# Layer 0 attention: every weight transposed on VectorE, and half of the minimum's input folded on GpSimd

## The chip, the cores and the metric

The kernel runs on one core of a Trainium2 chip. Five engines run side by side, each in the order of its own instruction list: TensorE (PE, with its weight loads shown as PEld), VectorE (DVE), ScalarE (ACT), GpSimd (POOL) and SyncE (SP), which here only issues DMAs. They meet at semaphores. The metric is the device time of one execution in microseconds (us).

## The reference

The whole program is a stack of four layers on an input of 2 x 256 channels x 1024 pixels. Only the attention of layer 0 is touched:

```python
qf = q.reshape(B * Hq * Wq_sp * NUM_HEADS, dk) / scale
kf = k.reshape(-1, dk)
vf = v.reshape(-1, dv)
A = jax.nn.softmax(qf @ kf.T, axis=1)
O = A @ vf
```

Queries and keys of both images and all four heads are thrown together: 8192 queries of 64 numbers against 8192 keys. After that come two more attentions, an additive attention and two mixtures of experts (layers 1 to 3), which are the same in both kernels.

## The kernel before

`layer0` normalises the input, projects it to `qT`, `kT` and `v`, and calls `shared_attention`, which is a software pipeline written out by hand. Queries are taken 32 positions at a time (`S` = 32), which makes 64 rows (`rows`), and each row is worked in four units (`units` = 256): `m` counts units, `i = m // 4` is the row, `p` picks a pair of heads, `h` picks half of the keys. One unit holds two score tiles of 128 x 1024, for r = 0 and r = 1 (the two heads of the pair). The softmax needs one minimum for a query (queries carry a minus sign), spread over four groups of 32 partitions.

What happens to a unit, in the order of its life:

- `score(m)`: 16 matmuls (L145; the trace has two instructions for each, 32) put the two tiles into PSUM. The pool `p_a` of tile r = 0 has two buffers, the pool `p_b` of tile r = 1 has one. DVE copies tile 0 to SBUF and takes its minimum on the way (L152); ACT copies tile 1 (L155). The copies (`sc0`, `sc1`) have 7 buffers each.
- `reduce(m)`: DVE takes the minimum of tile 1 over its 1024 columns (L166). After the second unit of a pair (h = 1), `gather` sends four small DMAs on SP's queue (L161), which bring the minima of the four partition groups side by side into `sa_got`.
- `spread_least(k)`: DVE reduces `sa_got` to `sa_min` (L172), and four DMAs on SP (L175) copy the result to all partition groups as `sa_shift`.
- `weigh(m)`: ACT takes the exponential of both tiles in place with `sa_shift` as bias (L182), and sums it.
- `turn(m)`: DVE transposes the first 768 of the 1024 columns of both tiles in blocks of 32 x 32 (L195). `turn_late(m)`: PE transposes the last 256 columns (L203, four instructions) into PSUM, and ACT copies them out to `wl` (L204).
- `value(m)`: 16 matmuls (32 instructions, L221) multiply weights and values into `sums`. Columns that PE transposed come out in another order, so they need values in that order too, `v_odd`, which `layer0` makes ahead of the attention (L364 to L377: four GpSimd copies, 32 PE instructions, 8 DVE additions).
- Once in a row: the sums of the weights are gathered with four DMAs (from `weigh`, `sa_sums`), inverted (`invert`, L228, L229, and L232 on GpSimd), spread by a matmul (L238) and copied by ACT (L243). `done` multiplies them in on DVE (L394); every eighth row it also projects the output (L400, L405).

A manual schedule fixes the order on every engine. At step n the calls are issued in the order of the loop at the end of `shared_attention`, each for a unit some steps back. Before, that loop calls `done(n-13)`, `reduce(n-1)`, `turn(n-6)`, `weigh(n-5)`, `score(n)`, `turn_late(n-6)`, `spread_least` of the pair that ended at n-2, `invert(n-10)`, `value(n-9)` and `spread(n-12)`. So a pair of units 2k and 2k+1 has its last `reduce`, with the gather, in step 2k+2, and its `spread_least` in step 2k+3. In that step the DVE has `reduce(2k+2)`, two transposes and the copy of the scores before it comes to the reduction that needs the gathered minima.

Of the kernel before, what the change touches and what calls it, by code (L numbers as in the profile page):

```python
# [19 lines left out]
F32 = mybir.dt.float32  # L20
# [3 lines left out]
ALU = mybir.AluOpType  # L24
AX = mybir.AxisListType
PSUM = bass.MemoryType.PSUM

P = 128
B, C, N = 2, 256, 1024
T = B * N  # L30
NT = T // P
CC = C // P
CH = 512
# [36 lines left out]
class Stack:  # L70
# [34 lines left out]

    def shared_attention(self, qT, kT, v, v_odd, ctx, done):

# [7 lines left out]


        tc, nc = self.tc, self.nc
        S, G, B, LATE = 32, P // 32, N // 32, 8
        DIRECT = (B - LATE) * S
        rows = T // S
        units = 4 * rows
        psum = lambda name, bufs: ctx.enter_context(tc.tile_pool(name=name, bufs=bufs, space=PSUM))
        p_a, p_b, p_o, p_t = psum("sa_a", 2), psum("sa_b", 1), psum("sa_o", 1), psum("sa_t", 1)
        sb = ctx.enter_context(tc.tile_pool(name="sa_sb", bufs=2))
        keys = kT.rearrange("p n (b c i) -> p n b c i", c=G, i=S)  # L130
        ones = sb.tile([S, P], F32, name="ones", bufs=1)
        nc.gpsimd.memset(ones, 1.0)
        names = "least got shift total parts scores weights late sums rec norm"
        least, got, shift, total, parts, scores, weights, late, sums, rec, norm = ({} for _ in names.split())

        def score(m):
            i, p, h = m // 4, m // 2 % 2, m % 2
# [19 lines left out]
        def gather(t, n, name):  # L157
# [3 lines left out]
                nc.sync.dma_start(out=g[:, :, c, :], in_=t[S * c : S * (c + 1)])  # L161
            return g.rearrange("q n c h -> q n (c h)")

        def reduce(m):
            h = m % 2
            nc.vector.tensor_reduce(least[m // 2][:, 1, h : h + 1], scores[m][1], AX.X, ALU.min)  # L166
            if h == 1:
                got[m // 2] = gather(least.pop(m // 2), 2, "sa_got")

        def spread_least(k):  # L170
            t = self.small.tile([S, 2], F32, name="sa_min")
            nc.vector.tensor_reduce(t, got.pop(k), AX.X, ALU.min)  # L172
            shift[k] = self.small.tile([P, 2], F32, name="sa_shift")
            for c in range(G):
                nc.sync.dma_start(out=shift[k][S * c : S * (c + 1)], in_=t)  # L175

        def weigh(m):
            i, p, h = m // 4, m // 2 % 2, m % 2
            if m % 4 == 0:
                total[i] = self.small.tile([P, 4, 2], F32, name="sa_total")  # L180
            for r in range(2):
                nc.scalar.activation(  # L182
                    scores[m][r], scores[m][r], AF.Exp, bias=shift[m // 2][:, r : r + 1], scale=-1.0,
                    accum_out=total[i][:, 2 * p + r, h : h + 1],
                )
            if m % 4 == 3:
                parts[i] = gather(total.pop(i), 4, "sa_sums")

        def turn(m):
            i, p, h = m // 4, m // 2 % 2, m % 2  # L190
            if p == 0:
                weights[i, h] = sb.tile([P, 4, DIRECT], F32, name="wt", bufs=3)
                late[i, h] = sb.tile([P, LATE // 4, 4, P], F32, name="wl", bufs=3)
            for r in range(2):
                nc.vector.transpose(weights[i, h][:, 2 * p + r, :], scores[m][r][:, :DIRECT])  # L195

        def turn_late(m):
            i, p, h = m // 4, m // 2 % 2, m % 2
            ps = p_t.tile([P, LATE // 4, 2, P], F32, name="ps_t")
            for r, s in enumerate(scores.pop(m)):  # L200
                for g in range(LATE // 4):
                    at = DIRECT + g * P
                    nc.tensor.transpose(ps[:, g, r, :], s[:, at : at + P], self.ident)  # L203
            return lambda: nc.scalar.copy(late[i, h][:, :, 2 * p : 2 * p + 2, :], ps)  # L204

        def value(m):
            i, h, j = m // 4, m // 2 % 2, m % 2
            if h == 0 and j == 0:
                sums[i] = p_o.tile([P, 4, S], F32, name="ps_o")
            for t in range(B // 4):  # L210
                for k in range(2):
                    b = B // 2 * k + B // 4 * j + t
                    at = B * h + b
                    if b < B - LATE:
                        values = v[:, at % NT, 64 * (at // NT) : 64 * (at // NT + 1)]
                        w = weights[i, h][:, :, S * b : S * (b + 1)]
                    else:
                        g, c = t // G, t % G
                        values = v_odd[:, h, t, :]
                        w = late[i, h][:, g, :, S * c : S * (c + 1)]  # L220
                    nc.tensor.matmul(  # L221
                        sums[i][64 * k : 64 * (k + 1)], lhsT=values, rhs=w,
                        start=(h == 0 and j == 0 and t == 0), stop=(h == 1 and j == 1 and t == B // 4 - 1),
                    )

        def invert(i):
            t, r = (self.small.tile([S, 4], F32, name=f"sa_{n}") for n in ("tot", "rec"))
            nc.vector.tensor_reduce(t, parts.pop(i), AX.X, ALU.add)  # L228
            nc.vector.reciprocal(r, t)  # L229
            rec[i] = sb.tile([S, 4, S], F32, name="diag")  # L230
            shape = [S, 4, S]
            nc.gpsimd.tensor_tensor(  # L232
                rec[i], self.ident[0:S, 0:S].unsqueeze(1).to_broadcast(shape), broadcast(r, shape), ALU.mult
            )

        def spread(i):
            ps = p_t.tile([P, 4, S], F32, name="ps_n", tag="ps_t")
            nc.tensor.matmul(  # L238
                ps.rearrange("p n q -> p (n q)"), lhsT=ones, rhs=rec.pop(i).rearrange("p n q -> p (n q)"),
                start=True, stop=True,  # L240
            )
            norm[i] = sb.tile([P, 4, S], F32, name="norm")
            nc.scalar.copy(norm[i], ps)  # L243

        with tc.manual_schedule():
            for n in range(units + 14):
                on = lambda d: 0 <= n - d < units
                row = lambda d: on(d) and (n - d) % 4 == 0
                if row(13):
                    i = (n - 13) // 4  # L250
                    done(i, sums.pop(i), norm.pop(i), p_t)
                if on(1):
                    reduce(n - 1)
                if on(6):
                    turn(n - 6)
                if on(5):
                    weigh(n - 5)
                if on(0):
                    score(n)
                if on(6):  # L260
                    turn_late(n - 6)()
                if on(3) and (n - 3) % 2 == 0:
                    spread_least((n - 3) // 2)
                if row(10):
                    invert((n - 10) // 4)
                if on(9):
                    value(n - 9)
                if row(12):
                    spread((n - 12) // 4)

    def layer0(self, xT):
        tc, nc = self.tc, self.nc
        with ExitStack() as ctx:
            w = ctx.enter_context(tc.tile_pool(name="l0_w", bufs=1))
            big = ctx.enter_context(tc.tile_pool(name="l0_big", bufs=1))


            qT = big.tile([P, CC, T], F32, name="qT")  # L280
            kT = big.tile([P, 4, T], F32, name="kT")
            v = big.tile([P, NT, C], F32, name="v")
            v_odd = big.tile([P, 2, 8, 64], F32, name="v_odd")

            with tc.tile_pool(name="l0_xn", bufs=1) as xp, tc.tile_pool(
                name="l0_ps", bufs=4, space=PSUM
# [74 lines left out]
                    nc.vector.tensor_tensor(v[:, i, :], ps, bv, ALU.add)  # L361


                late = xp.tile([P, CC, 2, 4, 4, 32], F32, name="late")  # L364
                runs = xn[:, :, N:].rearrange("p c (g b r i) -> p c g b r i", g=2, b=4, r=4)
                for c in range(CC):
                    for g in range(2):
                        nc.gpsimd.tensor_copy(late[:, c, g].rearrange("p r b i -> p b r i"), runs[:, c, g])
                for t in range(8):
                    ps = psum.tile([P, C], F32, name="ps_v", tag="ps_row")  # L370
                    for c in range(CC):
                        nc.tensor.matmul(
                            ps, lhsT=late[:, c, t // 4, t % 4].rearrange("p b i -> p (b i)"), rhs=wv[:, c, :],
                            start=(c == 0), stop=(c == CC - 1),
                        )
                    odd = lambda a: a.rearrange("p (h r d) -> p h r d", h=2, r=2)[:, :, 1, :]
                    nc.vector.tensor_tensor(v_odd[:, :, t, :], odd(ps), odd(bv), ALU.add)  # L377


            zero = big.tile([P, C], F32, name="zero")  # L380
            nc.gpsimd.memset(zero, 0.0)
            for slots in self.slots_in:
# [21 lines left out]
                    x = xT[:, o, t * C : (t + 1) * C]  # L404
                    nc.vector.scalar_tensor_tensor(x, ps, bo[:, o : o + 1], x, ALU.add, ALU.add)  # L405

            self.shared_attention(qT, kT, v, v_odd, ctx, done)

    def pool_stats(self, pool, psum, mv, average, tag="ps_row"):

# [1445 lines left out]
```

## Time and profile before

| what | us |
|---|---|
| median of 3 timed runs | 2989.76 (2987.06 to 2990.24) |
| the profiled execution, its time | 2959.93 |
| the profiled execution, its span | 2958.2 |
| from the first score matmul to the last output of layer 0's attention | 67.6 to 1275.4 |
| busy in the whole span: PE, DVE, ACT, POOL | 2756.9, 1952.9, 1945.6, 429.5 |

The profile is of one execution, and all durations below come from it. A row of the trace shows the start, the duration, the engine, the line in the kernel, the operation, output and input tiles with their shapes, and in brackets how long the engine sat idle before it and what ended that. An instruction starts before the one ahead of it has fully ended, so the spacing from start to start is what one instruction costs a busy engine, and is less than its duration. PE's busy time counts modelled ends and doesn't say that it works at its peak.

Layer 0's attention takes some 41% of the span.

### The profile page before, as it was taken

The numbers are of one execution on the slowest core, as the hardware profiler recorded it, in microseconds if no ns is written. First come the engines' busy times: TensorE is split into PE (matmuls) and PEld (weight loads), VectorE is DVE, ScalarE is ACT, GpSimd is POOL, SyncE is SP. The second block draws the span as 40 slices with busy tenths as digits, with TensorE's granted clock in tenths as the row PEclk, the third lists the DMA queues.
The fourth block names the chain that finished last, engine by engine and source line by source line (L and its number), as shares of the span: only waits on it lengthen the run. The fifth ranks groups of instructions, "written<-read, shape, count | busy, mean of one in ns | idle before, by whom it ended". The sixth has DMA issues, their size and how long they took to land. (4 is left out here: it accounts for less than half of the span.)

```text
span 2958.2 us, 78693 instructions
## 1 busy us (share of the span) xinstructions
PE 2756.9 (93%) x33062; PEld 1743.4 (59%) x33062; DVE 1952.9 (66%) x3650; ACT 1945.6 (66%) x2941; POOL 429.5 (15%) x538
## 2 busy tenths in 40 slices
PE   7999999999999999979999968699999999999997
PEld 4465656666666656655565445499866634355586
DVE  5898989898989898847778956663522234224242
ACT  1787878787878887825555522121199898998732
POOL 4000000000000000000111123433411120302142
PEclk9999999999999999989999988799999999999998
DMA  3000000000000000011101010243312210312254
GB/s 130 2 3 3 3 3 3 3 3 3 3 3 3 3 3 3 3 48 31 27 14 31 6 27 1 95 161 107 116 64 64 69 35 1 146 58 85 94 196 126
DMA packets 180578, 131.46 MB, mean 44 GB/s; under 512 B 130992, under 2 KB 162368, under 8 KB 173056
## 3 DMA queue, kind: packets, MB, share of 16 engines
q0 software_dynamic: 29232, 81.71, 8.3%
q1 hardware_dynamic: 149552, 44.27, 6.7%
q8 instruction: 259, 4.24, 0.6%
q14 instruction: 95, 0.78, 0.1%
q10 hardware_dynamic: 1440, 0.47, 0.1%
HBM read 181.24 MB, written 29.49 MB: 71 GB/s over the span
## 5 line engine op out<-in xcount | busy, mean ns | idle before, releaser
L182 ACT ACTIVATE sc<-sc,sa_shift 128x1024 f32<-128x1024 f32 x512 | 585.2, 1148 | 54.3 <-DMA sa_shift<-sa_min 54.1
L1641 ACT ACTIVATE th<-kT,qb 128x1024 f32<-128x1024 f32 x512 | 539.6, 1134 | 49.7 <-PE ps_e L1650 43.6
L145 PE MATMUL ps_s<-kT,qT 64*32 64x512 f32 x8192 | 505.0, 597 | 9.2 <-ACT sc L155 8.5
L221 PE MATMUL ps_o<-wt,v 128*64 128x128 f32 x6144 | 503.2, 276 | 0.0
L221 PEld LDWEIGHTS ps_o<-wt,v 128*64 128x64 f32 x6144 | 442.1, 137 | 42.7 <-issue 42.7
L195 DVE STREAM_TRANSPOSE wt<-sc 128x768 f32<-128x768 f32 x512 | 465.7, 943 | 0.9 <-ACT sc L182 0.9
L155 ACT COPY sc<-ps_s 128x1024 f32<-128x1024 f32 x256 | 257.4, 1005 | 117.9 <-PE ps_s L145 43.7
L1423 PEld LDWEIGHTS ps_h<-xe,ew 128*128 128x128 f32 x2320 | 276.1, 194 | 56.6 <-issue 32.8
L166 DVE TENSOR_REDUCE sa_least<-sc 128x1 f32<-128x1024 f32 x256 | 306.1, 1196 | 1.6 <-ACT sc L155 1.5
L152 DVE TENSOR_SCALAR_CACHE_REDUCE sc<-ps_s 128x1024 f32<-128x1024 f32 x256 | 301.3, 1177 | 6.4 <-PE ps_s L145 6.4
L1650 PE MATMUL ps_e<-th,pick 128*32 128x512 f32 x2048 | 299.5, 611 | 5.8 <-DVE sc_a L1657 4.4
L1423 PE MATMUL ps_h<-xe,ew 128*128 128x128 f32 x2320 | 292.1, 280 | 7.9 <-DVE xe L1406 7.9
L1443 PE MATMUL ps_y<-ew,h 128*128 128x256 f32 x1160 | 271.5, 383 | 3.5 <-DVE y L1447 2.1
L221 PE MATMUL ps_o<-wl,v_odd 128*64 128x128 f32 x2048 | 251.8, 276 | 0.0
L1443 PEld LDWEIGHTS ps_y<-ew,h 128*128 128x128 f32 x1160 | 212.9, 190 | 60.7 <-issue 18.8
L145 PEld LDWEIGHTS ps_s<-kT,qT 64*32 64x32 f32 x8192 | 126.8, 106 | 201.0 <-issue 169.0
L203 PEld LDWEIGHTS ps_t<-ident,sc 128*128 128x128 f32 x1024 | 107.8, 141 | 216.5 <-issue 168.6
L649 ACT ACTIVATE sc<-sc,l_least 128x1024 f32<-128x1024 f32 x128 | 146.7, 1147 | 126.9 <-DVE sc L636 126.5
L221 PEld LDWEIGHTS ps_o<-wl,v_odd 128*64 128x64 f32 x2048 | 221.2, 137 | 0.0
L1434 DVE TENSOR_TENSOR hb<-ps_h,ew 128x512 f32<-128x512 f32 x115 | 79.4, 690 | 198.2 <-PE ps_h L1423 172.3
L232 POOL TENSOR_TENSOR diag<-ident,sa_rec 32x128 f32<-32x128 f32 x64 | 24.9, 390 | 1172.1 <-DVE sa_rec L229 1172.1
L1412 ACT ACTIVATE h<-hb 128x512 f32<-128x512 f32 x115 | 71.5, 623 | 183.8 <-DVE hb L1434 183.6
(292 smaller groups left out, 3483.7 us busy)
## 6 DMA issues: line engine op xcount, KB each, us to landing
xr<-slots_in SPq DMA_DIRECT2D x99, 128.0 KB, 2.8
slots_out<-y SPq DMA_DIRECT2D x99, 128.0 KB, 1.7
sa_got<-sa_least SPq DMA_DIRECT2D x512, 0.5 KB, 1.8
sa_shift<-sa_min SPq DMA_DIRECT2D x512, 0.2 KB, 1.7
slots_in<-zero POOLq DMA_DIRECT2D x46, 128.0 KB, 2.2
sa_sums<-sa_total SPq DMA_DIRECT2D x256, 1.0 KB, 1.8
kh<-kh SPq DMA_DIRECT2D x32, 128.0 KB, 2.3
qh<-qh SPq DMA_DIRECT2D x32, 128.0 KB, 2.3
```

The source lines that it names most:

```text
L145: nc.tensor.matmul(ps[r][S * c : S * (c + 1), a, :].rearrange("p (b i) -> p b i", i=S), lhsT=qT[half, p, S * i : S * (i + 1)], rhs=keys[ha ...
L152: nc.vector.tensor_scalar(scores[m][0], flat[0], 1.0, None, ALU.mult, ALU.min, accum_out=least[m // 2][:, 0, h : h + 1])
L155: nc.scalar.copy(scores[m][1], flat[1])
L166: nc.vector.tensor_reduce(least[m // 2][:, 1, h : h + 1], scores[m][1], AX.X, ALU.min)
L182: nc.scalar.activation(scores[m][r], scores[m][r], AF.Exp, bias=shift[m // 2][:, r : r + 1], scale=-1.0, accum_out=total[i][:, 2 * p + r, ...
L195: nc.vector.transpose(weights[i, h][:, 2 * p + r, :], scores[m][r][:, :DIRECT])
L221: nc.tensor.matmul(sums[i][64 * k : 64 * (k + 1)], lhsT=values, rhs=w, start=(h == 0 and j == 0 and t == 0), stop=(h == 1 and j == 1 and t ...
L649: nc.scalar.activation(scores[n][r], scores[n][r], AF.Exp, bias=least[n][:, r : r + 1], scale=-1.0, accum_out=total[n // 4][:, at : at + 1],)
L1423: nc.tensor.matmul(ps[:, j, :], lhsT=a[:, c, at : at + P], rhs=x[:, c, :], start=(c == 0), stop=(c == CC - 1),)
L1443: nc.tensor.matmul(ps, lhsT=h[:, j, :], rhs=w2[:, j, :], start=(j == 0), stop=(j == HB - 1))
L1641: nc.scalar.activation(h, keys, AF.Tanh, bias=self.qb[b][:, s // G, g : g + 1])
L1650: nc.tensor.matmul(pe[i][c * U : (c + 1) * U, a, :], lhsT=self.pick[:, k, :], rhs=h[:, a, :], start=(k == 0), stop=(k == G - 1),)
```

## The change

All 1024 columns are transposed on DVE; `turn_late`, the PSUM tile it used, ACT's copy of it, `wl` and `v_odd` go. In their place GpSimd folds tile 1 of each unit in half: for the left half a and the right half b it computes a - min(max(a - b, 0), 3e38), which is the smaller of the two, in three instructions of 128 x 512. DVE's `reduce` then runs over 512 columns and not over 1024. In the schedule `fold(n)` stands right after `score(n)`; `reduce` moves from n-1 to n-3 and behind the score; `spread_least` moves to the pair that ended at n-3, and all later calls move back by one step.

```diff
+        def fold(m):
+            x = scores[m][1]
+            a, b = x[:, :CH], x[:, CH:]
+            folded[m] = y = sb.tile([P, CH], F32, name="fold", bufs=3)
+            nc.gpsimd.tensor_tensor(y, a, b, ALU.subtract)
+            nc.gpsimd.tensor_scalar(y, y, 3.0e38, 0.0, ALU.min, ALU.max)
+            nc.gpsimd.tensor_tensor(y, a, y, ALU.subtract)
+
         def reduce(m):
             h = m % 2
-            nc.vector.tensor_reduce(least[m // 2][:, 1, h : h + 1], scores[m][1], AX.X, ALU.min)
+            nc.vector.tensor_reduce(least[m // 2][:, 1, h : h + 1], folded.pop(m), AX.X, ALU.min)
             if h == 1:
                 got[m // 2] = gather(least.pop(m // 2), 2, "sa_got")
...
             if p == 0:
-                weights[i, h] = sb.tile([P, 4, DIRECT], F32, name="wt", bufs=3)
-                late[i, h] = sb.tile([P, LATE // 4, 4, P], F32, name="wl", bufs=3)
-            for r in range(2):
-                nc.vector.transpose(weights[i, h][:, 2 * p + r, :], scores[m][r][:, :DIRECT])
-
-        def turn_late(m):
...
+                weights[i, h] = sb.tile([P, 4, N], F32, name="wt", bufs=3)
+            for r, x in enumerate(scores.pop(m)):
+                nc.vector.transpose(weights[i, h][:, 2 * p + r, :], x)
...
-            for n in range(units + 14):
+            for n in range(units + 15):
...
-                if row(13):
-                    i = (n - 13) // 4
+                if row(14):
+                    i = (n - 14) // 4
                     done(i, sums.pop(i), norm.pop(i), p_t)
-                if on(1):
-                    reduce(n - 1)
+                if on(7):
+                    turn(n - 7)
                 if on(6):
-                    turn(n - 6)
-                if on(5):
-                    weigh(n - 5)
+                    weigh(n - 6)
                 if on(0):
                     score(n)
-                if on(6):
-                    turn_late(n - 6)()
-                if on(3) and (n - 3) % 2 == 0:
-                    spread_least((n - 3) // 2)
-                if row(10):
-                    invert((n - 10) // 4)
-                if on(9):
-                    value(n - 9)
-                if row(12):
-                    spread((n - 12) // 4)
+                    fold(n)
+                if on(3):
+                    reduce(n - 3)
+                if on(4) and (n - 4) % 2 == 0:
+                    spread_least((n - 4) // 2)
+                if row(11):
+                    invert((n - 11) // 4)
+                if on(10):
+                    value(n - 10)
+                if row(13):
+                    spread((n - 13) // 4)
```

More of the change, by code (lines that the diff above doesn't have):

```diff
@@ L104, in rsqrt, with shared_attention @@
         return r
-    def shared_attention(self, qT, kT, v, v_odd, ctx, done):
+    def shared_attention(self, qT, kT, v, ctx, done):
         tc, nc = self.tc, self.nc
-        S, G, B, LATE = 32, P // 32, N // 32, 8
-        DIRECT = (B - LATE) * S
+        S, G, B = 32, P // 32, N // 32
         rows = T // S
@@ L132, in shared_attention @@
         nc.gpsimd.memset(ones, 1.0)
-        names = "least got shift total parts scores weights late sums rec norm"
-        least, got, shift, total, parts, scores, weights, late, sums, rec, norm = ({} for _ in names.split())
+        names = "least folded got shift total parts scores weights sums rec norm"
+        least, folded, got, shift, total, parts, scores, weights, sums, rec, norm = ({} for _ in names.split())
         def score(m):
@@ L191, in turn @@
             if p == 0:
-                weights[i, h] = sb.tile([P, 4, DIRECT], F32, name="wt", bufs=3)
-                late[i, h] = sb.tile([P, LATE // 4, 4, P], F32, name="wl", bufs=3)
-            for r in range(2):
-                nc.vector.transpose(weights[i, h][:, 2 * p + r, :], scores[m][r][:, :DIRECT])
-        def turn_late(m):
[L198 to L204, printed above, removed]
+                weights[i, h] = sb.tile([P, 4, N], F32, name="wt", bufs=3)
+            for r, x in enumerate(scores.pop(m)):
+                nc.vector.transpose(weights[i, h][:, 2 * p + r, :], x)
         def value(m):
@@ L213, in value @@
                     at = B * h + b
[L214 to L220, printed above, removed]
                     nc.tensor.matmul(
-                        sums[i][64 * k : 64 * (k + 1)], lhsT=values, rhs=w,
+                        sums[i][64 * k : 64 * (k + 1)],
+                        lhsT=v[:, at % NT, 64 * (at // NT) : 64 * (at // NT + 1)],
+                        rhs=weights[i, h][:, :, S * b : S * (b + 1)],
                         start=(h == 0 and j == 0 and t == 0), stop=(h == 1 and j == 1 and t == B // 4 - 1),
@@ L282, in layer0 @@
             v = big.tile([P, NT, C], F32, name="v")
-            v_odd = big.tile([P, 2, 8, 64], F32, name="v_odd")
             with tc.tile_pool(name="l0_xn", bufs=1) as xp, tc.tile_pool(
@@ L361, in layer0 @@
                     nc.vector.tensor_tensor(v[:, i, :], ps, bv, ALU.add)
[L364 to L377, printed above, removed]
             zero = big.tile([P, C], F32, name="zero")
@@ L405, in done @@
                     nc.vector.scalar_tensor_tensor(x, ps, bo[:, o : o + 1], x, ALU.add, ALU.add)
-            self.shared_attention(qT, kT, v, v_odd, ctx, done)
+            self.shared_attention(qT, kT, v, ctx, done)
     def pool_stats(self, pool, psum, mv, average, tag="ps_row"):
```

## The prediction, made before the changed kernel was run

> **What bounds the kernel now.** I read the busy times of each engine over the attention first, then one row of the pipeline on PE and on DVE in order of time, then the waits. The attention alone:
>
> ```profile
> 67.30:1275.40 1208.10, 1183.51 (x17664) 719.27 (x17664) 1076.22 (x1618) 979.17 (x1602) 25.53 (x67) 1.00 0.05 3
> ```
>
> The columns are PE, PEld, DVE, ACT and POOL busy, the granted clock, DMA. PE is busy for 98% at full clock, POOL for 2%. In order of time on PE:
>
> ```profile
> 599.53 0.48 PE L238 MATMUL ps_n<-diag,ones 32*128 32x128 f32 x2
> 599.94 1.95 PE L145 MATMUL ps_s<-kT,qT 64*32 64x512 f32 x32
> 601.82 0.66 PE L203 MATMUL ps_t<-ident,sc 128*128 128x128 f32 x4
> 602.40 1.97 PE L221 MATMUL ps_o<-wt,v 128*64 128x128 f32 x32
> 604.30 1.95 PE L145 MATMUL ps_s<-kT,qT 64*32 64x512 f32 x32
> ```
>
> No row has an idle time ahead of it. From start to start a unit costs 1.88 + 0.58 + 1.90 = 4.36 us, and once a row L238 adds 0.41: 4 x 4.36 + 0.41 = 17.85 us a row. On DVE:
>
> ```profile
> 600.35 0.29 DVE L394 TENSOR_TENSOR oT<-ps_o,norm 128x128 f32<-128x128 f32 x1 [1.10 <-ACT norm L243]
> 600.55 1.21 DVE L166 TENSOR_REDUCE sa_least<-sc 128x1 f32<-128x1024 f32 x1
> 601.68 1.83 DVE L195 STREAM_TRANSPOSE wt<-sc 128x768 f32<-128x768 f32 x2
> 603.43 1.18 DVE L152 TENSOR_SCALAR_CACHE_REDUCE sc<-ps_s 128x1024 f32<-128x1024 f32 x1
> 604.55 0.08 DVE L152 DVE_READ_ACCUMULATOR sc<-ps_s 128x1 f32 x1
> 604.55 0.15 DVE L172 TENSOR_REDUCE sa_min<-sa_got 32x2 f32<-32x16 f32 x1
> 604.63 1.20 DVE L166 TENSOR_REDUCE sa_least<-sc 128x1 f32<-128x1024 f32 x1
> 605.76 1.81 DVE L195 STREAM_TRANSPOSE wt<-sc 128x768 f32<-128x768 f32 x2
> ```
>
> DVE is nearly as full: its one wait in a row is 1.10 us for the norm, the end of PE's chain. Its own work is 17.86 - 1.10 = 16.76 us a row (L394 stands at 1193.15, 1211.01 and 1228.88). So PE sets the pace, with DVE 6% behind. L172 needs four DMAs, but it stands 1.5 steps behind the reduction that sends them, and waits for nothing.
>
> **What goes.** On PE four transposes, 0.58 us a unit: 3.78 us are left, 15.5 a row. On ACT L204, 0.59: two exponentials at 1.15 and a copy at 0.9 are left, 3.2 a unit. Ahead of the attention L372 goes, 7.07 us of PE time between the values and the first score, which waits for it: about -6.9 us, once.
>
> **DVE's own work.** The transposes grow from 768 to 1024 columns. The pair of 768 takes 1.75 us from start to start; layer 1 has the same instruction at 1024, a pair busy for 2.37 with 1.23 for the second, so 1.14 to 1.17 each and 2.30 a pair: +0.55 a unit. The reduction shrinks: 1024 columns cost 1.13 start to start, and the step from 768 to 1024 columns gives 1.04 ns a column, so 512 cost 1.13 - 0.53 = 0.60: -0.53. (L901 has a 128x512 reduction of 684 ns alone.) Together about nothing: 4.02 us a unit (2.30 + 1.12 + 0.60). With L172 at 0.08 twice, L228 and L229 at 0.36 and L394 at 0.20 a row that is 16.8 us: without any new wait DVE would bound at 16.8 and PE would not.
>
> **The new wait.** Here I expect the change to lose. `reduce(m)` runs at step m+3 and `spread_least(k)` at step 2k+4, so for m = 2k+1 both are in the same step, and the built order confirms it: DVE's L178 (`sa_min`) stands directly behind the L172 (`reduce`) whose result SP must gather. DVE waits for a whole round trip of four DMAs, with nothing between, once in two units. Three rows bound it:
>
> ```profile
> 1244.23 2.58 SPq L161 DMA_DIRECT2D sa_got<-sa_least  x4
> 1248.12 0.16 DVE L172 TENSOR_REDUCE sa_min<-sa_got 32x2 f32<-32x16 f32 x1 [1.22 <-DMA sa_got<-sa_least]
> ...
> 80.44 2.47 SPq L175 DMA_DIRECT2D sa_shift<-sa_min  x4
> 84.05 1.28 ACT L182 ACT_TABLE_LOAD   x1 [0.76 <-DMA sa_shift<-sa_min]
> ...
> 83.01 3.40 SPq L161 DMA_DIRECT2D sa_got<-sa_least  x4
> 87.72 0.16 DVE L172 TENSOR_REDUCE sa_min<-sa_got 32x2 f32<-32x16 f32 x1 [1.12 <-DMA sa_got<-sa_least]
> ```
>
> At the end of the attention the waiting DVE started 3.89 us after the first of the four issues, and an issue follows DVE's end by 0.03 (80.41 to 80.44): 3.92. The low end is the second pair: `sa_min` ended at 80.41, ACT went on at 84.05, 3.64. The high end is the third: 87.72 - 83.01 + 0.03 = 4.74, where an issue was slow. Over the attention a group of four issues takes 2.75 us in the mean, not 2.58; I take half of that excess and get 4.0.
>
> What is queued behind the wait: the next transposes, so the copy that empties `ps_s`, so PE. A pair of units then costs DVE 4.02 in the odd step and 2.30 + 1.12 + 0.68 + 4.0 + 0.08 = 8.18 in the even one (the reduction's full 0.68, since nothing overlaps its end): 12.20. A row: 24.40 + 0.36 + 0.20 = 24.96 against 17.86, +7.10 us, and 64 rows make +454. The 1.10 for the norm is inside the 17.86 and vanishes, as PE now runs ahead.
>
> **What is hidden, and by what.** All else fits under 6.1 us a unit: PE 3.9, ACT 3.2, SP five groups of 2.75 in 24.96. GpSimd's `fold` is two two-input instructions of 128x512, 1.36 us apart in layer 1 (L700 to L701), and a clip that no row shows. From below 0.47 (half of a 128x1024 memset at 0.94), from above 1.28 (the two-input form); I take the copy of 128x512, 0.86: 3.6 us a unit. The result is needed three steps later, so up to 6.1 us costs nothing. New order dependences: ACT's copy of tile 1 reuses a buffer that the transposes of the same step read, so copy (1.0) and next score (1.95) follow the transposes. Counted from the start of a pair's odd step that chain ends at 2.3 + 0.1 + 1.0 + 1.95 = 5.4, and DVE comes to those scores at 4.02 + 2.30 = 6.3: hidden by 0.9. Without that cover it costs what it is late.
>
> GpSimd beside DVE: layer 1 has this already.
>
> ```profile
> 1381.01 1.28 POOL L700 TENSOR_TENSOR oT<-half,half 128x512 f32<-128x512 f32 x1 [13.11 <-issue]
> 1382.37 1.28 POOL L701 TENSOR_TENSOR oT<-oT,spread 128x512 f32<-128x512 f32 x1
> ...
> 1382.63 2.37 DVE L655 STREAM_TRANSPOSE wt<-sc 128x1024 f32<-128x1024 f32 x2
> ```
>
> Transposes and GpSimd arithmetic overlap and neither is longer than elsewhere (L655 1225 ns and L701 1281 in the mean). So I charge nothing. The Trainium skill speaks against the change here: Perfetto Trace Analysis, section Optimizing Scalar/DVE Operations, says that GpSimd and DVE share an SBUF read port, so that moving work between the two might not help. If GpSimd's 3.6 us were taken from DVE, that alone would be an estimated +0.9 ms; the rows show none of it for these forms.
>
> **The sum.** +454 for the rows, -7 for `v_odd`, and +5 for a drain that has two round trips more in series: +452. On the profiled execution's 2959.93 that is 3412. The timed runs of before lie 30 us above that one execution (median 2989.76), and I add the difference to the median: **3442 us**.
>
> **Rivals.** *PE goes cold.* With a pair at 12.2 us PE has some 4 us without work in each. Before, one such gap:
>
> ```profile
> 88.66 3.46 PE L145 MATMUL ps_s<-kT,qT 64*32 64x512 f32 x30 [3.37 <-ACT sc L155]
> ...
> 90.00:92.00 2.00, 2.00 (x22) 0.26 (x7) 1.60 (x2) 0.88 (x2) 0.00 (x0) 0.50 0.04 1
> ```
>
> After 3.37 us idle the clock fell to 0.50 and the scores took 3.46 and not 1.95. In the even step that is 0.6 late after 0.9 of slack: 128 x 0.6 = +77, so 3519. Against: after shorter gaps the clock stayed at 1.00, and it was back 3.4 us later. TensorE: Matmul & The Clock Gate (Trainium skill), section on the HAM clock gate, has PE fall to half clock after an idle window of about 3.4 us that runs freely; by it only some of the gaps would hit, an estimated third of the 77.
>
> *GpSimd becomes the bound*, if the clip takes over 3.4 us (6.1 - 2.72) or the two engines do hinder each other. At a clip of 5 us a unit costs 7.7: 256 x (7.7 - 4.46) = +830, some 3820. The layer 1 rows speak against it.
>
> *The round trip is hidden, faster.* If it cost DVE less than (17.86 - 16.8) / 2 = 0.53 us a pair, DVE's 16.8 us a row would decide: 64 x -1.06 - 7 = -75, 2915. For it: PE loses 13% of its work and before the same reduction waited for nothing. Against it: there is no instruction between the two reductions, and one of these DMAs alone takes 1.8 us to land.
>
> **How the numbers follow.** Forecast 0.78, cold PE 0.12, GpSimd 0.06, hidden 0.03, no change 0.01. Range: a round trip of 3.64 gives 128 x -0.36 = -46, 3396; of 4.74 +95, 3537; the cold PE's 3519 lies inside. I take 3390 to 3535. A difference of 0.2% (6 us) is about what a measurement of this kernel can tell: faster 0.03, same 0.01, slower 0.96.
>
> **What would show it.** Right: DVE's `sa_min` L178 waits about 4.0 us for `sa_got` DMAs, 128 times, some 500 us in all; PE's busy share in the attention falls to some 65%; rows are 25 us apart; the 512 reduction takes 0.68 and the transposes 1.2; POOL is busy 3.6 us a unit. Wrong: a wait under 0.5 us there, a reduction or a transpose that is longer beside GpSimd, a DVE wait for PE's scores (cold PE) or for POOL in every step.

## The result, and the profile after

| what | before | after |
|---|---|---|
| median of 4 timed runs each, side by side, us | 2988.41 (2981.41 to 2990.24) | 3518.97 (3514.08 to 3527.91) |
| the profiled execution, its time, us | 2959.93 | 3527.91 |
| layer 0's attention in the profile, us | 67.6 to 1275.4: 1207.8 | 62.5 to 1802.9: 1740.4 |
| waits of DVE for `sa_got`, us | 0 in the steady part | 547.0 in 128 waits |

The ratio is 1.1784 [1.1753, 1.1815]. By the medians the kernel became slower by 530.6 us, and in the profiles the attention alone by 532.6, so the whole loss lies there. The two profiled executions themselves lie 568 us apart: some 40 of that stand behind the attention (1682.8 us before, 1723.3 after), where the kernels are the same. That is not the change: in e5 below, the changed kernel again, the attention takes 1738.8 us and the rest behind it 1680.9.

DVE in order of time, over one pair of units (start, duration, engine, line, operation, tiles; in brackets the idle time before and what ended it):

```profile
587.15 1.22 DVE L150 TENSOR_SCALAR_CACHE_REDUCE sc<-ps_s 128x1024 f32<-128x1024 f32 x1 [0.40 <-PE ps_s L143]
588.30 0.08 DVE L150 DVE_READ_ACCUMULATOR sc<-ps_s 128x1 f32 x1
588.30 0.68 DVE L172 TENSOR_REDUCE sa_least<-fold 128x1 f32<-128x512 f32 x1
593.53 0.16 DVE L178 TENSOR_REDUCE sa_min<-sa_got 32x2 f32<-32x16 f32 x1 [4.55 <-DMA sa_got<-sa_least]
593.62 2.35 DVE L200 STREAM_TRANSPOSE wt<-sc 128x1024 f32<-128x1024 f32 x2
...
597.82 2.35 DVE L200 STREAM_TRANSPOSE wt<-sc 128x1024 f32<-128x1024 f32 x2
600.74 1.23 DVE L150 TENSOR_SCALAR_CACHE_REDUCE sc<-ps_s 128x1024 f32<-128x1024 f32 x1 [0.57 <-PE ps_s L143]
```

L172 sends the gather and L178 reads it, with nothing between them on DVE: 4.55 us idle. The first and the last row have short waits for PE's scores, 0.40 and 0.57 us, which the kernel before had 7 times in its whole attention (6.4 us in all). The same stretch on SP's queue and on PE:

```profile
589.00 3.22 SPq L159 DMA_DIRECT2D sa_got<-sa_least  x4
593.71 2.46 SPq L181 DMA_DIRECT2D sa_shift<-sa_min  x4
```

```profile
593.06 1.04 PE L143 MATMUL ps_s<-kT,qT 64*32 64x512 f32 x2
597.12 3.52 PE L143 MATMUL ps_s<-kT,qT 64*32 64x512 f32 x30 [3.01 <-ACT sc L153]
600.57 1.97 PE L210 MATMUL ps_o<-wt,v 128*64 128x128 f32 x32
602.46 1.95 PE L143 MATMUL ps_s<-kT,qT 64*32 64x512 f32 x32
```

The four issues of this gather took 3.22 us, where four quick ones take 2.5. PE stood still for 3.01 us and then needed 3.52 for 30 of the 32 score instructions that otherwise take 1.95. The waits over the attention (who waited for whom, us in total, times, longest):

```profile
ACT sc L153 <- DVE wt L200: 733.0, 179, 9.3
DVE sa_min L178 <- DMA sa_got<-sa_least: 547.0, 128, 5.9
...
PE ps_s L143 <- ACT sc L153: 347.0, 125, 6.6
...
DVE xT L378 <- PE ps_out L373: 54.1, 16, 3.9
...
DVE sc L150 <- PE ps_s L143: 37.6, 64, 2.3
```

The first three are one chain: DVE waits for its DMAs, so its transposes are late, so ACT's copy, which reuses the buffer that they read, is late, so PE gets no free `ps_s`. The busy times by stretch (length, then PE, PEld, DVE, ACT, POOL busy, granted clock, DMA share, GB/s), first the whole attention, then a stretch in PE's gap and one behind it:

```profile
62.50:1802.90 1740.40, 1337.70 (x16640) 697.16 (x16640) 1089.85 (x1617) 866.39 (x1346) 833.25 (x833) 0.88 0.03 2
594.00:596.00 2.00, 0.11 (x1) 0.00 (x0) 2.00 (x3) 0.00 (x0) 0.00 (x0) 1.00 0.02 0
598.00:600.00 2.00, 2.00 (x30) 0.40 (x14) 2.00 (x2) 1.66 (x4) 1.83 (x3) 0.50 0.10 2
```

Before, PE was busy for 98% at clock 1.00. Now no engine is full: PE 77%, DVE 63%. The clock falls to 0.50 behind the gap, and its mean over the attention is 0.88. Each operation by itself costs about what rows of before gave: 1225 ns for this transpose in layer 1, 1281 for GpSimd's two-input form there, 1176 for the copy with the minimum (groups of after: busy and mean ns, then idle time before it):

```profile
L200 DVE STREAM_TRANSPOSE wt<-sc 128x1024 f32<-128x1024 f32 x512 | 602.0, 1209 | 0.8 <-ACT sc L188 0.8
L166 POOL TENSOR_TENSOR fold<-sc 128x512 f32<-128x512 f32 x256 | 328.6, 1283 | 826.3 <-DVE sa_least L172 501.1 <-DVE sa_tot L219 307.7 <-ACT sc L153 6.5
L150 DVE TENSOR_SCALAR_CACHE_REDUCE sc<-ps_s 128x1024 f32<-128x1024 f32 x256 | 304.4, 1189 | 38.0 <-PE ps_s L143 37.6
L172 DVE TENSOR_REDUCE sa_least<-fold 128x1 f32<-128x512 f32 x256 | 172.4, 673 | 0.0
```

### The profile page after: what moved, and what is told of

The parts are those of the page before. It is cut to its first block, busy times and chain, and to the rows that moved or that the text cites. A ratio compares the mean times of both kernels' runs of the same rounds, so it can differ in the third digit from the quotient of the medians.

```text
span 3526.2 us, 77338 instructions
## 1 busy us (share of the span) xinstructions
PE 2924.4 (83%) x32006; PEld 1722.0 (49%) x32006; DVE 1963.4 (56%) x3642; ACT 1834.1 (52%) x2685; POOL 1234.1 (35%) x1302
## 5 line engine op out<-in xcount | busy, mean ns | idle before, releaser
L143 PE MATMUL ps_s<-kT,qT 64*32 64x512 f32 x8192 | 750.2, 706 | 350.2 <-ACT sc L153 347.0
L166 POOL TENSOR_TENSOR fold<-sc 128x512 f32<-128x512 f32 x256 | 328.6, 1283 | 826.3 <-DVE sa_least L172 501.1
L210 PEld LDWEIGHTS ps_o<-wt,v 128*64 128x64 f32 x8192 | 482.4, 146 | 275.8 <-issue 218.4
L200 DVE STREAM_TRANSPOSE wt<-sc 128x1024 f32<-128x1024 f32 x512 | 602.0, 1209 | 0.8 <-ACT sc L188 0.8
L210 PE MATMUL ps_o<-wt,v 128*64 128x128 f32 x8192 | 542.3, 289 | 11.6 <-DVE oT L367 11.6
L143 PEld LDWEIGHTS ps_s<-kT,qT 64*32 64x32 f32 x8192 | 160.2, 116 | 701.6 <-ACT sc L153 474.3
L168 POOL TENSOR_TENSOR fold<-sc,fold 128x512 f32<-128x512 f32 x256 | 325.5, 1272 | 21.4
L150 DVE TENSOR_SCALAR_CACHE_REDUCE sc<-ps_s 128x1024 f32<-128x1024 f32 x256 | 304.4, 1189 | 38.0 <-PE ps_s L143 37.6
L178 DVE TENSOR_REDUCE sa_min<-sa_got 32x2 f32<-32x16 f32 x128 | 20.1, 157 | 547.0 <-DMA sa_got<-sa_least 547.0
L628 DVE STREAM_TRANSPOSE wt<-sc 128x1024 f32<-128x1024 f32 x128 | 153.3, 1225 | 46.4 <-ACT sc L622 25.8
L609 DVE TENSOR_SCALAR_CACHE_REDUCE sc<-ps_s 128x1024 f32<-128x1024 f32 x128 | 150.6, 1212 | 39.5 <-PE ps_s L601 39.3
```

Source lines behind the costliest of these rows:

```text
L143: nc.tensor.matmul(ps[r][S * c : S * (c + 1), a, :].rearrange("p (b i) -> p b i", i=S), lhsT=qT[half, p, S * i : S * (i + 1)], rhs=keys[ha ...
L150: nc.vector.tensor_scalar(scores[m][0], flat[0], 1.0, None, ALU.mult, ALU.min, accum_out=least[m // 2][:, 0, h : h + 1])
L166: nc.gpsimd.tensor_tensor(y, a, b, ALU.subtract)
L168: nc.gpsimd.tensor_tensor(y, a, y, ALU.subtract)
L200: nc.vector.transpose(weights[i, h][:, 2 * p + r, :], x)
L210: nc.tensor.matmul(sums[i][64 * k : 64 * (k + 1)], lhsT=v[:, at % NT, 64 * (at // NT) : 64 * (at // NT + 1)], rhs=weights[i, h][:, :, S * ...
```

## The experiments

Each ratio is to the kernel before, run on the same chip beside the experiment; its median was 2957.07 for e1 to e4, 2957.64 for e5 to e8 and 2993.49 for e9 and e10. All edits are made to the changed kernel, except e8, which is made to the kernel before. The theory is that the wait for the round trip sets the time; the rivals are that PE's half clock, or the engines' own work (GpSimd beside DVE), does.

### e1: the reduction one step earlier

```diff
-                if on(3):
-                    reduce(n - 3)
+                if on(2):
+                    reduce(n - 2)
```

> The changed kernel with reduce(n-2) in place of reduce(n-3), at the same place in the step: the gather goes out one step before spread_least. Theory 1 (the round trip of the gather is exposed, 547 us of waits at sa_min): about 4.0 us of other work now lies between the two reductions, so the wait falls from 4.3 us to 0.3 to 0.6, the granted clock in the attention goes back to near 1.00, a row is 17.2 to 17.6 us, and the time 2920 to 2965. Theory 2 (VectorE is slowed by the longer transposes or by GpSimd working beside it): the wait at sa_min shrinks but the time comes back elsewhere on VectorE, and the kernel stays above 3300.

Measured: 3011.61 us, ratio 1.0176 [1.0155, 1.0198]. Nine tenths of the loss went, with not one instruction less: the place of the reduction is the cause. But I missed the time by 47 us at the least, since some wait stayed, 114.9 us over the 128 pairs. SP's queue shows why, and below it DVE:

```profile
583.90 2.58 SPq L159 DMA_DIRECT2D sa_sums<-sa_total  x4
586.58 3.03 SPq L159 DMA_DIRECT2D sa_got<-sa_least  x4
```

```profile
584.64 0.67 DVE L172 TENSOR_REDUCE sa_least<-fold 128x1 f32<-128x512 f32 x1
...
590.92 0.16 DVE L178 TENSOR_REDUCE sa_min<-sa_got 32x2 f32<-32x16 f32 x1 [1.41 <-DMA sa_got<-sa_least]
```

The reduction ended at 585.3, but the gather was issued at 586.58, when the four issues of the sums ahead of it were done. In 62 of the 128 pairs the gather stood directly behind the sums like this, and the wait was 1.62 us in the mean; in the other 66 it was 0.22. I had counted the round trip from the reduction's end and forgotten what stands ahead of it in SP's queue.

### e2: the reduction one step earlier and first in its step

```diff
+                if on(2):
+                    reduce(n - 2)
                 if on(7):
                     turn(n - 7)
...
-                if on(3):
-                    reduce(n - 3)
```

> As the run before, but reduce(n-2) is the first thing in the step, ahead of the transposes, so that nearly two steps (7.4 us) lie between the gather and spread_least. Theory 1: no wait at sa_min at all, VectorE's own 16.8 us a row set the pace or slightly more where ScalarE's copy and TensorE follow, 2900 to 2945, and so faster than the kernel before the change. Theory 2: no better than the run before, above 3300.

Measured: 2923.89, ratio 0.9884 [0.9868, 0.9901]: faster than the kernel before. DVE in order of time:

```profile
591.74 1.17 DVE L150 TENSOR_SCALAR_CACHE_REDUCE sc<-ps_s 128x1024 f32<-128x1024 f32 x1
592.86 0.07 DVE L150 DVE_READ_ACCUMULATOR sc<-ps_s 128x1 f32 x1
592.86 0.15 DVE L178 TENSOR_REDUCE sa_min<-sa_got 32x2 f32<-32x16 f32 x1
592.94 0.66 DVE L172 TENSOR_REDUCE sa_least<-fold 128x1 f32<-128x512 f32 x1
593.53 2.35 DVE L200 STREAM_TRANSPOSE wt<-sc 128x1024 f32<-128x1024 f32 x2
...
597.55 0.29 DVE L367 TENSOR_TENSOR oT<-ps_o,norm 128x128 f32<-128x128 f32 x1 [0.54 <-ACT norm L234]
```

L178 waits for nothing any more (3.5 us in the whole attention); from the gather's first issue to L178 there are 5.9 us in the mean. A row takes 17.2 us (`oT` at 597.6 and 614.8) against 17.86 before, and the attention 1170.5, with the same GpSimd work as in the changed kernel. What is left of waiting in a row is again the norm, 0.54 us (40.4 in all).

### e3: the gather's four DMAs on two queues

```diff
-        def gather(t, n, name):
+        def gather(t, n, name, queues=(0, 0, 0, 0)):
...
-                nc.sync.dma_start(out=g[:, :, c, :], in_=t[S * c : S * (c + 1)])
+                (nc.sync, nc.scalar)[queues[c]].dma_start(out=g[:, :, c, :], in_=t[S * c : S * (c + 1)])
...
-                got[m // 2] = gather(least.pop(m // 2), 2, "sa_got")
+                got[m // 2] = gather(least.pop(m // 2), 2, "sa_got", (0, 1, 0, 1))
```

> The changed kernel with two of the four gather DMAs of sa_got issued from ScalarE's queue and two from SyncE's, nothing moved. Theory 1: the exposed round trip loses two issues, some 1.3 to 1.6 us of 4.3 in each pair, 128 x 1.3 to 1.6 = 165 to 205 us, and with a shorter gap on TensorE up to 40 us more: 3280 to 3355. Theory 2: the wait isn't the price, within 30 us of 3519. Theory 3 (ScalarE is then held up by the issues, which wait for VectorE): less than 100 us are gained and the waits of VectorE for ScalarE's exponentials appear.

Measured: 3341.76, ratio 1.1301 [1.1282, 1.1319], which is (1.1766 - 1.1301) x 2957 = 137 us below the changed kernel (its ratio in e5 is used). The wait fell from 547.0 to 424.3 us, 0.96 a pair. The direction is as the theory has it, the size less than I expected. Here is one pair:

```profile
594.86 2.59 SPq L159 DMA_DIRECT2D sa_got<-sa_least  x2
594.87 1.26 ACTq L159 DMA_DIRECT2D sa_got<-sa_least  x2
...
599.03 0.16 DVE L178 TENSOR_REDUCE sa_min<-sa_got 32x2 f32<-32x16 f32 x1 [4.20 <-DMA sa_got<-sa_least]
```

Two issues on ACT's queue took 1.26 us, but the two on SP took 2.59 here, as long as four quick ones. That is one of 26 pairs with an issue of over 0.9 us on SP, and such pairs are not the whole reason: the median wait, too, fell only from 3.91 to 2.94 us. The DMAs landed later: from the start of the last issue to L178 the median went from 1.90 to 2.27 us. The third theory (ACT held up by its issues) doesn't explain it: ACT did stand idle at 117 exponentials, 252.6 us in all, but DVE waited 0.7 us for them.

### e4, e5, e6: PE kept busy

```diff
+        def warm():
+            ps = p_t.tile([P, 4, P], F32, name="ps_w", tag="ps_t")
+            for j in range(12):
+                nc.tensor.matmul(ps[:, j % 4, :], lhsT=self.ident, rhs=self.ident, start=True, stop=True)
...
+                if on(10) and n % 2 == 1:
+                    warm()
```

> The changed kernel with 12 matmuls of the identity with itself (some 2.5 us) put on TensorE in each odd step, where it otherwise stands still; their result is not used. Theory 1a (of the 77 us above the forecast some 55 come from a half clock on TensorE after its gaps, 38 as waits for scores and 19 as waits for ps_out): the granted clock in the attention rises from 0.88 to above 0.97, VectorE's wait for ps_s nearly vanishes, and the time falls by 40 to 60 us to 3460 to 3480; the wait at sa_min stays at 4.2 us. Theory 1b (the clock costs nothing, all of it is the longer round trip): no change within 10 us, or slower by what the matmuls delay.

Measured: 3450.84, ratio 1.1667 [1.1646, 1.1688]. The changed kernel had not run beside it, so both went again side by side.

> The changed kernel itself once more, beside the kernels of this group on one chip: 17.5% to 18.2% above the kernel before, by every theory; it is the base for the next run.

> The kernel with 12 identity matmuls in each odd step, now on the same chip as the changed kernel. Theory 1a (the half clock after gaps costs some 55 us): 35 to 60 us below the changed kernel beside it. Theory 1b (it costs nothing): within 10 us of it.

Measured: e5 3481.95, ratio 1.1766 [1.1743, 1.1789]; e6 3457.18, ratio 1.1678 [1.1657, 1.1699]: 25 us less than e5, and less of a gain than I expected. In e6 the clock is back, and most of the wait stays:

```profile
62.70:1775.60 1712.90, 1596.02 (x19712) 1015.20 (x19712) 1083.40 (x1616) 866.14 (x1346) 834.84 (x832) 0.97 0.04 2
```

From e5 to e6 the DVE's waits for scores fall from 38.5 to 15.9 us and those for `ps_out` from 55.7 to 47.2, together -31; the waits for `sa_got` rise from 543.6 to 551.0, +7. That makes 24 of the 25.6 by which the attention became shorter (1738.8 to 1713.2). So the half clock is real, and taking most of it away gives back some 25 us of the 524. The clock is 0.97 and not 1.00 then, and what the added matmuls cost by themselves was not measured apart.

### e7: all transposes on DVE, no fold

The pipeline loop is that of the kernel before without `turn_late`, GpSimd's fold is gone, and `reduce` takes all 1024 columns:

```diff
-            nc.vector.tensor_reduce(least[m // 2][:, 1, h : h + 1], folded.pop(m), AX.X, ALU.min)
+            nc.vector.tensor_reduce(least[m // 2][:, 1, h : h + 1], scores[m][1], AX.X, ALU.min)
...
+                if on(1):
+                    reduce(n - 1)
+                if on(6):
+                    turn(n - 6)
...
-                if on(4) and (n - 4) % 2 == 0:
-                    spread_least((n - 4) // 2)
+                if on(3) and (n - 3) % 2 == 0:
+                    spread_least((n - 3) // 2)
```

> One part alone: all columns transposed on VectorE, no fold, reduction over 1024 columns, and the schedule of the kernel before. Theory 1: VectorE needs 4 x (2.30 + 1.12 + 1.13) + 0.16 + 0.36 + 0.20 = 18.9 us a row against 17.86 now, nothing is exposed, 64 x 1.06 - 7 = some 60 us above the kernel before. Theory 2 (the longer transposes are the loss): 300 us or more above it.

Measured: 3018.99, ratio 1.0200 [1.0183, 1.0217], +61 us, as expected. L178 waits 0.9 us in all. DVE is the bound here: it is busy for 1208 of the attention's 1281 us, and a row takes 18.8 us, close to DVE's 16.8 with the half reduction and 0.53 x 4 = 2.1 more.

### e8: the fold alone, with PE's transposes kept

The kernel before with `fold` (two buffers) and `reduce` over the fold, called first in the step:

```diff
-                if on(1):
-                    reduce(n - 1)
+                if on(2):
+                    reduce(n - 2)
...
                     score(n)
+                    fold(n)
```

> The other part alone: the kernel before with the fold on GpSimd (two buffers) and the reduction over 512 columns, as the first call of the step for n-2; transposes and all else as before, TensorE's included. TensorE keeps its 17.86 us a row; the gather has 2.9 us of work before its reduction, so some 1.4 us of wait a pair on VectorE, which has 2.1 us a row less to do. Theory 1: within -10 to +40 us of the kernel before. Theory 2 (GpSimd hinders VectorE): VectorE's reductions and transposes are longer than in the kernel before, 100 us or more above it.

Measured: 3009.68, ratio 1.0183 [1.0162, 1.0205], +52 us: outside what I expected, on the slow side. The waits of e8:

```profile
DVE sa_min L181 <- DMA sa_got<-sa_least: 192.7, 128, 3.4
...
ACT sc L191 <- DMA sa_shift<-sa_min: 155.8, 83, 4.1
PEld ps_t L212 <- ACT sc L191: 114.8, 137, 0.8
```

The wait for `sa_got` is 1.5 us a pair, as I had it. What I had not priced is the next link: `sa_shift` goes out later, ACT's exponentials wait 155.8 us for it (54.1 before), and PE's transposes, which stand right behind them, 114.8 (41.9 before). PE is still busy for 97% of the attention in this kernel, so that counts; that this chain is the whole of the 52 us was not tried by a run. The same two waits before:

```profile
ACT sc L182 <- DMA sa_shift<-sa_min: 54.1, 65, 3.0
...
PEld ps_t L203 <- ACT sc L182: 41.9, 50, 0.8
```

The groups settle the rival of GpSimd beside DVE, here in e8:

```profile
L204 DVE STREAM_TRANSPOSE wt<-sc 128x768 f32<-128x768 f32 x458 | 416.4, 942 | 0.0
...
L153 DVE TENSOR_SCALAR_CACHE_REDUCE sc<-ps_s 128x1024 f32<-128x1024 f32 x230 | 270.5, 1176 | 0.5 <-PE ps_s L146 0.5
```

And in the kernel before, with an idle GpSimd, over the same stretch:

```profile
L195 DVE STREAM_TRANSPOSE wt<-sc 128x768 f32<-128x768 f32 x477 | 433.7, 943 | 0.0
...
L152 DVE TENSOR_SCALAR_CACHE_REDUCE sc<-ps_s 128x1024 f32<-128x1024 f32 x238 | 279.8, 1176 | 0.0
```

The means are 942 and 943 ns, and 1176 and 1176: the fold hinders neither.

### e9, e10: what still waits in e2

e9 is e2 once more. e10 is e2 with the norm's matmul ahead of the row's value matmuls:

```diff
+                if row(13):
+                    spread((n - 13) // 4)
                 if on(10):
                     value(n - 10)
-                if row(13):
-                    spread((n - 13) // 4)
```

> The kernel with reduce(n-2) in front once more, as base for the next: 0.985 to 0.992 of the kernel before.

> As the run before, and spread(n-13) stands ahead of value(n-10) in the step, so that TensorE makes the norm before the last weighted sums of the step. With reduce(n-2) in front VectorE still waits 0.54 us a row for the norm (40 us in all). If VectorE alone sets the pace there, that wait goes and a row takes 16.8 us in place of 17.25: 15 to 30 us faster than the run before, 0.977 to 0.985 of the kernel before. If TensorE, which shows 397 us busy of 400 there, is the bound as well, the wait comes back as a wait for scores and the time stays within 6 us.

Measured: e9 2954.93, ratio 0.9871 [0.9856, 0.9887]; e10 2945.72, ratio 0.9830 [0.9814, 0.9847]. 9 us less, where I expected more: the wait for the norm went, and one for the value matmuls themselves (26.5 us in all, 0.33 at `oT` in place of 0.54) took its place. A row takes 17.02 us (607.79 to 624.81). This is the fastest kernel of the study, 1.7% below the kernel before.

## Why the prediction was right

**The wait.** Place, number and cause were right: L178, 128 times, a full round trip between two neighbours on DVE. e1 and e2 move only that reduction and take away nine tenths and all of the loss. Its size was a little low: 4.27 us a time, not 4.0, so 547 and not 512. Both lie inside the bounds of 3.64 and 4.74. 43 of the 128 gathers had a slow issue (3.19 us for four in the mean) and waited 4.49 us. Of the other 85 (2.55), 20 landed late, over 2.2 us after the start of the last issue, and waited 5.29; the remaining 65 waited 3.81, somewhat less than the 3.92 I took for a quick round trip. So the slow issues and the late landings add 0.46 us to the mean, where I had added 0.08: I had counted only the issues, at half their share, and no late landings. The last section says what both coincide with.

**The sum.** Of the 452, 459 were for the attention (454 for the rows and 5 for the drain) and -7 ahead of it. The attention grew by 532.6. Of the 74 that were missing, 35 are the longer wait, 37.6 - 6.4 = 31 the new waits for scores, which the centre had at 0, and 54.1 - 33.4 = 21 those for `ps_out`, which it left as they were. That makes 87, and 4 x 64 transposed pairs of 2.28 rather than 2.30 us take 5 back; some 8 too many remain unassigned. The rows stand at 571.37, 597.62, 624.11, 649.84 and 676.48: 26.3 us apart, not 25. Some 7 us were to go ahead of the attention, and its start moved by 67.6 - 62.5 = 5.1. The time fell 77 us above the forecast and 16 inside the range, and that owes something to luck: the range's upper end came from a longer wait alone, which was less than half of the miss.

**PE's half clock.** This was a rival at +77, and the measured 3519 is just its figure; yet that is a coincidence. The mechanism is there (clock 0.50, 3.52 us of scores), but it hits less often and less hard than the rival had it: behind the first eight, the changed kernel has 56 waits for scores of 0.43 us, not 128 of 0.6, and e6 gives back 25 us, a third of the 77. That third is also the estimate I had made with the Trainium skill, TensorE: Matmul & The Clock Gate, section on the HAM clock gate, by which the activity window runs freely, so that only some gaps would hit. The runs agree in size: of PE's 105 gaps of over 2 us ahead of scores, 62 were followed by scores at a mean clock under 0.6 and 23 by scores at full clock. They don't show that the phase of a window is the reason. The failing term is the charge of nothing in the centre.

**Busy times.** I forecast some 65% for PE; it is 77%, since the matmuls at half clock count as busy for twice as long. A mean clock of 0.88 means an estimated 0.12 x 1740 = 209 us of such extra busy time; without them PE would be busy for 1129 of 1740 us, 65%. The reduction (673 ns, forecast 680) and the transposes (1209, forecast 1200) were right. The clip takes 613 ns, not 860, so GpSimd needs 833 / 256 = 3.25 us a unit and not 3.6: it cost nothing here either way.

**The rivals that fell.** GpSimd as the bound: it is busy for 833 of 1740 us and waits for DVE, not DVE for it. Hindrance between the two: e8's rows show none. The Trainium skill (Perfetto Trace Analysis, Optimizing Scalar/DVE Operations) warns that moving work between the two might not help, as they share a read port; for these forms the rows show no such cost, and the measurement decides. The hidden round trip, 2915: wrong for this schedule, but it is what the change is worth once the schedule allows it. e2 and e10 come to 33 and 48 us below the kernel before, where I had worked out 75; DVE has short waits at the end of each row.

## What to carry to other kernels

When two instructions on one engine are joined by a DMA round trip, look at what stands between them in that engine's order after a change of schedule: moving the producer by two steps and the consumer by one turned a covered round trip into 4.3 us of standstill, 128 times. Give it the whole trip, counted from the queue's place and not from the producer's end, since other DMAs may be ahead of it (1.4 us more in half of e1's pairs). And judge a shift of work between engines apart from the schedule that came with it: with e2's order of calls the new division of work is 1.2% faster than the kernel before, and with its own it was 18% slower. (e10's 1.7% holds one more move, which the kernel before was not given.)

## What was not expected of the hardware

Some issues of small DMAs on SP take two to three times as long as the others, in every kernel. The issues of `sa_got` in the changed kernel (minimum, median and maximum in ns) and in the kernel before:

```profile
L159 SPq DMA_DIRECT2D sa_got<-sa_least x512: 585/595/1737, 79.0 to 1776.0; - x171
```

```profile
L161 SPq DMA_DIRECT2D sa_got<-sa_least x512: 586/612/1767, 75.2 to 1246.2; - x171
```

39 of the 512 take over 900 ns after the change and 32 of 512 before it; in the other runs it is 20 to 48. The traces show what they coincide with. The profile's page of the changed kernel lists a DMA queue that it calls `instruction` (packets, MB, share of the 16 DMA engines):

```profile
q8 instruction: 251, 4.11, 0.5%
```

Its packets have 16 KB and take 1.1 us in the mean during the attention. In the trace's list of packets, all 39 slow issues of `sa_got` overlap one of them, and all 32 of the kernel before; of the 473 and 480 others only 44 and 29 do. In all twelve traces no slow issue of `sa_got` is without one. In the changed kernel a slow issue ends 0.37 to 0.42 us after the packet. The late landings go with the same packets: in all 20 gathers that had quick issues and landed late, one lies between the first issue and L178, against 2 of the 65 that were neither. That the packets are the cause is not shown, since no run moved them. Where a round trip is exposed, these delays are paid for: 0.46 x 128 = 59 of the 547 us.
